# A graph attention kernel: the load of `a` moved to another queue ahead of the first head's weights, and the transposes of the last tile placed one product sooner

## The chip, the cores and the metric

The kernel runs on one core of one Trainium2 chip. The metric is the device time of the whole kernel in microseconds (us). The kernel before took 2300.03 us, the median of four runs (2299.52 to 2300.47).

A core has five engines that run side by side and wait for each other through semaphores: PE (matrix products; PEld is its loading of weights, which overlaps with products), DVE and ACT (elementwise work; ACT also does exponentials), POOL (elementwise work on SBUF) and SP (which only issues transfers). ACT and POOL issue transfers too. The profile numbers the transfer queues: q1 is SP's, q10 is ACT's, q0 is POOL's. All of them feed the same 16 DMA engines.

## The reference

The input `x` has 128 batches of 64 nodes with 512 features, `adj` is a 64 x 64 mask, and all arithmetic is float32. Cut to what matters:

```
h = relu(layernorm(x))
# four heads
Wh = einsum('bnf,hfo->bhno', h, W_heads)              # W_heads [4, 512, 512]
e = leaky(Wh @ a[:, :512] (rows) + Wh @ a[:, 512:] (columns))   # a_heads [4, 1024]
attn = softmax(where(adj > 0, e, -1e9))
h1 = elu(attn @ Wh), heads side by side               # [128, 64, 2048]
# one head
out = elu(the same with W_out [2048, 512] and a_out)
y = relu(out @ w1 + b1) @ w2 + b2 + out
result = x + layernorm(y) * gamma + beta
```

The scores need only `h @ (W a)`, so the kernel folds `a` into the weights first: eight columns `W_h a` for the four heads and the two halves of `a`.

## The kernel before

The 8192 rows of `x` are worked in 64 tiles of 128 rows, and these in 16 groups of four tiles. In a group, PE first does the projections of the four heads (`project1`, line 289 for its matmuls), then the output head's product (`project2`, line 304), and beside it the feed-forward layers of the group before. The products are done by a scheme with seven partial products, so sums of weight blocks are made once on POOL (`weight_sums`), written to DRAM and read back piece by piece (`piece`, line 220).

The first group is different, and the change lies there. Its heads are done with plain products, `head_w(m, j)` (line 629: four matmuls by head m's weights for tile j, which the profile counts as eight), because the blocks of weights are not summed yet. The order in the code is written out by hand at the end of the kernel (from line 852 on) and a scheduler keeps it on each engine by and large: an engine works its instructions strictly in order.

What happens at the start, by name:

- `load(t)` (line 107) brings tile t of `x` through SP's queue. `X[0]` is issued first, then `ar`, then `X[1]` to `X[3]`.
- `ar` (lines 112 to 114) is a 128 x 512 tile, zeroed by DVE; its first eight rows are then loaded with the two halves of `a` for each of four heads (8 rows of 2 KB, 16 KB).
- `fetch(m)` (lines 163 to 169) loads a whole weight matrix of 1 MB, `pw` in the profile. Head 0's goes through ACT's queue, heads 1 to 3 through SP's, the later ones through POOL's. In the text they are called pw0, pw1, pw2, pw3. An argument `after` makes the issue wait for another instruction, by the helper `behind` (line 73), which adds a dependence through a semaphore.
- `norm1(t)` makes the layer norm's statistics on DVE (lines 326 to 332), two small steps on POOL (334, 344) and `hn` by one activation on ACT (346).
- `spread_a(m)` (line 177) spreads two rows of `ar` over all partitions by two products with a column of the identity; they need `ar`. `fold(m, ab)` (line 188) multiplies pw m by them on DVE and sums into the columns of `wa`.
- `transpose_h(t)` (lines 362 and 364) transposes tile t of `hn` by four small PE matmuls into `pth` and copies it to `hT` on ACT. `head_w(m, t)` needs that copy.
- `masks()` (lines 137 to 153) makes small tables on DVE, held behind the last fold: among them `isq` and `hsf`.
- `project_f(0)` (line 372) multiplies `wa` by the four `hT` and spreads the result by ACT into `L` (line 380) and `R` (385), which need `isq` and `hsf`. `scores1(0)` (405) and the softmax follow.

PE's order there is: spread_a(0), transpose_h(0), spread_a(1), head_w(0,0), transpose_h(1), spread_a(2), head_w(0,1), transpose_h(2), spread_a(3), head_w(0,2), transpose_h(3), head_w(0,3), head_w(1,0), project_f(0), head_w(1,1), scores1(0), and so on.

Each transfer through SP's and ACT's queues takes the next of eight semaphores, so an issue waits until the transfer that had the same semaphore before it has landed.

Of the kernel before, what the change touches and what calls it, by code (L numbers as in the profile page):

```python
# [22 lines left out]
def gat_preln_kernel(  # L23
# [30 lines left out]
    nc = tc.nc  # L54
    P = 128
    B, N, F = x.shape
    H = W_heads.shape[0]
    O = W_heads.shape[2]
# [21 lines left out]
    def bank(name):  # L80
        return ps.tile([P, 2, T], FP, tag="mm", name=name)

    def flat(ap):
        return ap.rearrange("p a b -> p (a b)")

    def behind(ins, after, reason):
        tc.add_manual_dep(
            ins.ins, after.ins.name,
            mybir.DependencyInfo(mybir.DependencyClass.Sync, mybir.DependencyReason.DATA),
            reason=reason,  # L90
        )

    def aux(shape, name):
        return ps.tile(shape, FP, tag="aux", name=name, bufs=2)
# [16 lines left out]

    ar = wk.tile([P, O], FP, tag="elu", name="ar", bufs=3)
    nc.vector.memset(ar, 0.0)
    nc.sync.dma_start(out=ar[0:2 * H], in_=a_heads.rearrange("h (r p) -> (h r) p", p=O))
    for t in range(1, G):
        X[t] = load(t)
    aj = const.tile([P, N], mybir.dt.int32, name="aj")
# [45 lines left out]
    def fetch(m, after=None):  # L163
        MT[m] = big.tile([P, KC, O], FP, tag=homes[m], name=f"pw{m}")
        queue = nc.scalar if m == 0 else nc.sync if m < H else nc.gpsimd
        ins = queue.dma_start(out=MT[m], in_=mats[m].rearrange("(k p) o -> p k o", p=P))
        if after is not None:
            behind(ins, after, "not in front of what is needed first")
        return ins

    def spread_a(m, after=None):

        ab = []
        for c in range(2):
            pb = flat(bank(f"pab{m}_{c}"))
            r = 2 * m + c
            ins = nc.tensor.matmul(pb, ident[:, r:r + 1].to_broadcast([P, P]), ar, start=True, stop=True)
            if after is not None:
                behind(ins, after, "not in front of it")
            ab.append(pb)  # L180
        return ab

    def fold(m, ab):

        for c in range(2):
            for k in range(KC):
                junk = wk.tile([P, O], FP, tag="t", name=f"jk{c}_{m}_{k}")
                LAST["fold"] = nc.vector.scalar_tensor_tensor(
                    junk, MT[m][:, k, :], 1.0, ab[c], ALU.mult, ALU.mult,
                    accum_out=wa[:, k, c * H + m:c * H + m + 1],  # L190
                )

    def weight_sums(m, after=None):

        w = MT[m]
        b11, b12 = w[:, 0:2, 0:Q], w[:, 0:2, Q:O]
        b21, b22 = w[:, 2:4, 0:Q], w[:, 2:4, Q:O]
        tag = ("ot", "rt")[m % 2]
        s = [big.tile([P, 2, 2, Q], FP, tag=f"{tag}{i}", name=f"pt{m}_{i}") for i in range(2)]
        free = [nc.gpsimd.tensor_tensor(s[0][:, 0], b12, b11, ALU.subtract)]  # L200
        nc.gpsimd.tensor_tensor(s[0][:, 1], b22, s[0][:, 0], ALU.subtract)
        free.append(nc.gpsimd.tensor_tensor(s[1][:, 0], b22, b12, ALU.subtract))
        for ins in free if after is not None else ():
            behind(ins, after, "the sums come behind it")
        last = nc.gpsimd.tensor_tensor(s[1][:, 1], b21, s[0][:, 1], ALU.subtract)
        TC[m] = [dram.tile([P, 2, 2, Q], FP, name=f"tc{m}_{i}") for i in range(2)]
        for i in range(2):
            nc.gpsimd.dma_start(out=TC[m][i], in_=s[i])
        return last
# [149 lines left out]
    def transpose_h(t):  # L359
        pt = aux([P, KC, P], f"pth{t}")  # L360
        for k in range(KC):
            LAST["th"] = nc.tensor.transpose(pt[:, k, :], HN[t][:, ts(k, P)], ident)
        HT[t] = wk.tile([P, KC, P], FP, tag="hT", name=f"hT{t}", bufs=4)
        LAST["hT"] = nc.scalar.copy(HT[t], pt)
# [261 lines left out]
    def head_w(m, j):  # L626
        pb = aux([P, O], f"hw{m}_{j}")
        for k in range(KC):
            LAST["pe"] = LAST["hw", m, j] = nc.tensor.matmul(
                pb, HT[j][:, k, :], MT[m][:, k, :], start=k == 0, stop=k == KC - 1  # L630
            )
        nc.scalar.copy(flat(HW[j][:, m]), pb)
# [217 lines left out]


    for m in range(H):
        fetch(m)
    nc.vector.memset(wa, 0.0)
    norm1(0)
    ab = spread_a(0)
# [14 lines left out]
    head_w(0, 1)  # L871
    transpose_h(2)
    fold(3, spread_a(3, LAST["pe"]))
    weight_sums(1, LAST["nb"])
    weight_sums(2, LAST["nb"])
    head_w(0, 2)
    transpose_h(3)
    head_w(0, 3)
    masks()
    head_w(1, 0)  # L880
# [150 lines left out]
```

## Time and profile before

| | us |
|---|---|
| median of four runs | 2300.03 |
| the profiled execution | 2299.52 |
| its span on the core | 2297.5 |
| PE busy in the span | 2274.5 |
| DVE busy | 1280.5 |
| POOL busy | 1018.6 |
| ACT busy | 904.4 |
| DMA engines, mean rate over the span | 157 GB/s |
| DMA engines, mean rate 6.49 to 36 us | 341 GB/s |

The profile is of one execution. A row of the timeline gives the start, the length, the engine, the line of the code, the operation, what it writes and reads, and in brackets how long the engine had been idle before and what ended that. The length of a matmul row holds its passage through the array, so rows of PE overlap; the distance of the starts tells the pace. A row of the waits gives the waiting engine and line, what it waited for, the total in us, how many times, and the longest.

Transfers of the first 40 us, with the time from issue to landing:

```profile
pw<-in_L_gnn_W_heads_dram SPq DMA_DIRECT2D x3, 1024.0 KB, 10.2
x<-in_x_dram SPq DMA_DIRECT2D x8, 256.0 KB, 6.0
pw<-in_L_gnn_W_heads_dram ACTq DMA_DIRECT2D x1, 1024.0 KB, 6.3
ar<-in_L_gnn_a_heads_dram SPq DMA_DIRECT2D x1, 16.0 KB
```

Their issues:

```profile
0.72 0.47 ACTq L166 DMA_DIRECT2D pw<-in_L_gnn_W_heads_dram  x1
0.73 0.39 SPq L107 DMA_DIRECT2D x<-in_x_dram  x1
1.41 0.36 SPq L114 DMA_DIRECT2D ar<-in_L_gnn_a_heads_dram  x1
1.81 1.36 SPq L107 DMA_DIRECT2D x<-in_x_dram  x3
3.22 4.17 SPq L166 DMA_DIRECT2D pw<-in_L_gnn_W_heads_dram  x3
```

### The profile page before, as it was taken

How to read it: one execution, taken by the hardware profiler on the slowest of the kernel's cores; microseconds unless marked ns; L12 is line 12 of the kernel's file. 1: busy time of each engine (PE TensorE's matmuls, PEld its weight loads, DVE VectorE, ACT ScalarE, POOL GpSimd, SP SyncE). 2: the span in 40 equal slices, each digit the busy share in tenths (PEclk: the TensorE clock that was granted, in tenths of full speed). 3: DMA queues.
4: the chain of work that ended last, by engine and by line, in shares of the span. 5: the costliest groups of instructions: out<-in, count | busy, mean ns of one | idle time of the engine just before them, and what ended most of it. 6: DMA issues, size and time to landing. Idle time of an engine off the chain costs nothing. (4 is left out here: it accounts for less than half of the span.)

```text
span 2297.5 us, 33255 instructions
## 1 busy us (share of the span) xinstructions
PE 2274.5 (99%) x11856; PEld 1890.6 (82%) x11856; DVE 1280.5 (56%) x2226; ACT 904.4 (39%) x1633; POOL 1018.6 (44%) x906
## 2 busy tenths in 40 slices
PE   8999999999999999999999999999999999999997
PEld 4688888888888888888888888888888888888885
DVE  7555554755546555564655546555475554744427
ACT  3435344252442525335253352534425244251512
POOL 7653534435254442644425344353444525533324
PEclk9999999999999999999999999999999999999999
DMA  7554464644546455464544645446464454635543
GB/s 280 197 179 132 145 180 132 183 133 143 178 132 184 136 152 165 133 184 133 163 152 140 181 134 177 132 146 180 132 181 133 145 176 131 184 118 169 162 146 106
DMA packets 255011, 361.14 MB, mean 157 GB/s; under 512 B 23768, under 2 KB 143608, under 8 KB 254848
## 3 DMA queue, kind: packets, MB, share of 16 engines
q1 hardware_dynamic: 249744, 341.16, 49.2%
q0 software_dynamic: 4576, 16.81, 2.0%
q8 instruction: 96, 1.57, 0.3%
q10 hardware_dynamic: 528, 1.05, 0.1%
q14 instruction: 67, 0.55, 0.1%
HBM read 331.66 MB, written 27.26 MB: 156 GB/s over the span
## 5 line engine op out<-in xcount | busy, mean ns | idle before, releaser
L304 PE MATMUL g_b<-w,h 128*128 128x256 f32 x2560 | 593.1, 379 | 0.0
L304 PEld LDWEIGHTS g_b<-w,h 128*128 128x128 f32 x2560 | 481.1, 190 | 64.6 <-issue 2.0
L289 PE MATMUL g_a<-z,w 128*128 128x256 f32 x1440 | 341.7, 380 | 0.0
L289 PE MATMUL g_a<-zs_z,w 128*128 128x256 f32 x1440 | 336.0, 381 | 0.0
L289 PEld LDWEIGHTS g_a<-zs_z,w 128*128 128x128 f32 x1440 | 269.9, 190 | 59.2 <-issue 24.3
L289 PEld LDWEIGHTS g_a<-z,w 128*128 128x128 f32 x1440 | 272.3, 190 | 41.4 <-DVE g_a L603 5.0
L304 PE MATMUL g_b<-w,hS 128*128 128x256 f32 x1024 | 238.2, 379 | 0.0
L607 POOL TENSOR_TENSOR hS<-hS,h 128x512 f32<-128x512 f32 x60 | 78.1, 1302 | 360.3 <-DVE hS L573 360.3
L304 PEld LDWEIGHTS g_b<-w,hS 128*128 128x128 f32 x1024 | 192.1, 190 | 25.0 <-issue 0.2
L571 ACT ACTIVATE exc<-g_a 128x512 f32<-128x512 f32 x240 | 142.6, 594 | 164.9 <-DVE g_a L603 97.2
L573 DVE SCALAR_TENSOR_TENSOR h<-exc,g_a 128x512 f32<-128x512 f32 x180 | 123.5, 686 | 140.7 <-ACT exc L572 140.1
L572 ACT ACTIVATE exc<-exc 128x512 f32<-128x512 f32 x240 | 151.4, 631 | 6.6
L688 POOL TENSOR_TENSOR h<-h,h 128x512 f32<-128x512 f32 x64 | 86.8, 1364 | 138.6 <-PE g_b L304 138.6
L688 POOL TENSOR_TENSOR h<-hS,h 128x512 f32<-128x512 f32 x64 | 81.6, 1276 | 146.3 <-PE g_b L304 146.0
L314 POOL TENSOR_TENSOR zs_z<-zS,z 128x512 f32<-128x512 f32 x60 | 85.2, 1420 | 134.3 <-PE g_a L289 131.0
L489 ACT COPY at<-s1pt 128x512 f32<-128x512 f32 x64 | 34.4, 590 | 272.1 <-PE s1pt L485 272.1
L830 POOL TENSOR_TENSOR xr<-xr,bs 128x512 f32<-128x512 f32 x64 | 96.6, 1513 | 80.0 <-DMA xr<-in_x_dram 52.4
L304 PE MATMUL g_d<-w,rt 128*128 128x256 f32 x512 | 121.8, 380 | 2.2 <-DVE o L822 1.0
L289 PE MATMUL g_c<-ot,w 128*128 128x256 f32 x512 | 122.8, 383 | 0.6 <-DVE ot L792 0.6
L289 PE MATMUL g_a<-zS,w 128*128 128x256 f32 x480 | 113.4, 379 | 0.0
L304 PEld LDWEIGHTS g_d<-w,rt 128*128 128x128 f32 x512 | 96.9, 190 | 17.4 <-DVE o L822 2.3
L712 DVE SCALAR_TENSOR_TENSOR jf<-wh,ao 128x512 f32<-128x512 f32 x128 | 97.4, 797 | 23.8 <-ACT wh L694 23.6
(164 smaller groups left out, 3538.2 us busy)
## 6 DMA issues: line engine op xcount, KB each, us to landing
w<-tc SPq DMA_DIRECT2D x624, 256.0 KB, 2.8
w<-in_L_gnn_W_out_dram SPq DMA_DIRECT2D x192, 256.0 KB, 2.8
w<-in_L_gnn_W_heads_dram SPq DMA_DIRECT2D x180, 256.0 KB, 3.2
w<-in_L_gnn_w_dram SPq DMA_DIRECT2D x96, 256.0 KB, 2.8
x<-in_x_dram SPq DMA_DIRECT2D x64, 256.0 KB, 4.3
xr<-in_x_dram SPq DMA_DIRECT2D x128, 128.0 KB, 2.7
out_dram<-o SPq DMA_DIRECT2D x128, 128.0 KB, 2.4
tc<-pt POOLq DMA_DIRECT2D x20, 512.0 KB, 4.3
```

The lines of the kernel that those rows point to most:

```text
L289: LAST["pe"] = nc.tensor.matmul(bk[:, o, :], w[:, k, ts(o, P)], a[:, k, :], start=start and o == 0 and k == 0, stop=k == 1, skip_group_che ...
L304: LAST["pe"] = nc.tensor.matmul(bk[:, j, :], a[:, k, ts(j, P)], w[:, k, :], start=start and k == 0 and j == 0, stop=i == len(ms) - 1 and k ...
L314: eng.tensor_tensor(s2, s1, a11, ALU.subtract)
L489: nc.scalar.copy(AT[t].rearrange("p b h n -> p (b h) n"), pt)
L571: nc.scalar.activation(ex, src, AF.Relu, scale=-1.0)
L572: nc.scalar.activation(ex, ex, AF.Exp, scale=-1.0)
L573: nc.vector.scalar_tensor_tensor(dst, ex, -1.0, src, ALU.add, ALU.max)
L607: nc.gpsimd.tensor_tensor(dst, dst, H1["22"][:, h], ALU.add)
L688: nc.gpsimd.tensor_tensor(dst[:, h], x0[:, h], x1[:, h], ALU.subtract)
L712: nc.vector.scalar_tensor_tensor(junk, WH2[g][:, j], 1.0, ao[:, c, :], ALU.mult, ALU.mult, accum_out=f[:, c, j:j + 1],)
L830: nc.gpsimd.tensor_tensor(xr, xr, bs, ALU.add)
```

## The change

The load of `ar` is issued by ACT and not by SP. The load of head 0's weights, also issued by ACT, is made to wait for it. And `transpose_h(3)` is placed ahead of `weight_sums(1)`, `weight_sums(2)` and `head_w(0, 2)`; it stood behind them. What is computed is the same.

```diff
     ar = wk.tile([P, O], FP, tag="elu", name="ar", bufs=3)
     nc.vector.memset(ar, 0.0)
-    nc.sync.dma_start(out=ar[0:2 * H], in_=a_heads.rearrange("h (r p) -> (h r) p", p=O))
+    load_a = nc.scalar.dma_start(out=ar[0:2 * H], in_=a_heads.rearrange("h (r p) -> (h r) p", p=O))
     for t in range(1, G):
         X[t] = load(t)
...
     for m in range(H):
-        fetch(m)
+        fetch(m, load_a if m == 0 else None)
     nc.vector.memset(wa, 0.0)
     norm1(0)
     ab = spread_a(0)
...
     head_w(0, 1)
     transpose_h(2)
     fold(3, spread_a(3, LAST["pe"]))
+    transpose_h(3)
     weight_sums(1, LAST["nb"])
     weight_sums(2, LAST["nb"])
     head_w(0, 2)
-    transpose_h(3)
     head_w(0, 3)
     masks()
```

In the built program the order of instructions differs in these places alone. PE: the four transposes of tile 3 stand ahead of the eight matmuls of head_w(0,2). ACT: the load of `ar` stands first, pw0's second, and the copy of `hT` 3 ahead of the copy of head_w(0,2). SP: the load of `ar` is gone, and the first piece of W_out (line 220) stands ahead of the loads of tiles 5, 6 and 7 of `x`; it stood behind them. DVE: the statistics of tile 1 stand ahead of one small step (line 332) of tile 0.

## The prediction

> **What bounds the kernel now.** I read the page first (busy shares), then PE's idle time by stretches, then the waits of the first 40 us, then the timeline around the two places that the diff touches, and last the DMA queues in that stretch.
>
> ```profile
> PE 2274.5 (99%) x11856; PEld 1890.6 (82%) x11856; DVE 1280.5 (56%) x2226; ACT 904.4 (39%) x1633; POOL 1018.6 (44%) x906
> ...
> 0.00:6.49 6.49, 0.00 (x1) 0.03 (x1) 2.02 (x8) 1.40 (x2) 2.79 (x11) 1.00 0.72 243
> 6.49:36.00 29.51, 28.78 (x72) 13.26 (x72) 27.82 (x91) 7.42 (x12) 22.16 (x26) 1.00 0.96 341
> 36.00:600.00 564.00, 563.53 (x3025) 454.74 (x3024) 315.55 (x543) 234.04 (x431) 272.34 (x250) 1.00 0.53 163
> ...
> PE pab L177 <- DMA ar<-in_L_gnn_a_heads_dram: 6.5, 1, 6.5
> ...
> PE hw L629 <- ACT hT L364: 0.7, 1, 0.7
> ```
>
> The stretches list, after the length, the busy time of PE, PEld, DVE, ACT and POOL. PE is the bound: between 36 and 600 us it is idle for 564.00 - 563.53 = 0.47 us. The front holds two idle pieces: 6.49 us until the first matmul, ended by the landing of `ar`, and 0.73 us (29.51 - 28.78) in one wait, on the copy of a transposed h tile. So whatever brings PE's continuous run forward shifts the rest with it, and the two pieces are an upper limit of what this diff can give.
>
> ```profile
> 6.49 3.75 PE L177 MATMUL pab<-ar,ident 128*128 128x512 f32 x4 [6.49 <-DMA ar<-in_L_gnn_a_heads_dram]
> ...
> 10.03 1.06 PE L362 MATMUL pth<-ident,hn 128*128 128x128 f32 x4
> ...
> 10.89 2.29 PE L177 MATMUL pab<-ar,ident 128*128 128x512 f32 x4
> ...
> 13.02 3.60 PE L629 MATMUL hw<-pw,hT 128*128 128x512 f32 x8
> ...
> 27.63 0.60 PE L362 MATMUL pth<-ident,hn 128*128 128x128 f32 x4
> ...
> 28.31 0.59 ACT L364 COPY hT<-pth 128x512 f32<-128x512 f32 x1
> 28.95 0.30 PEld L629 LDWEIGHTS hw<-pw,hT 128*128 128x128 f32 x2 [0.96 <-ACT hT L364]
> ```
>
> From 6.49 to 13.02 PE works without a break: spread_a(0), the transposes of tile 0, spread_a(1), then head_w(0,0). That is 6.53 us. The weight loads of spread_a(0) start 0.86 apart, the last two of spread_a(1) 0.43 apart (11.73, 12.16), so the first 5.2 us ran at half pace, though the granted clock is printed as 1.00 there.
>
> **Part 2, transpose_h(3) before head_w(0,2).** Nothing is added or removed: four transposes and one copy change places with eight matmuls, and the copy of hT3 now comes before the copy of hw on ACT. Before, the transposes at 27.63 were followed by head_w(0,3), which needs their copy (28.31 + 0.59 = 28.90). At the sister place, tile 1, unrelated matmuls follow the transposes 0.44 later (16.45 to 16.89). So head_w(0,3) could start at 28.07 and starts at 28.95: 0.87 us (0.73 by the wait row, 0.96 by the weight loads' row). After, hT3's copy lies beside the 3.43 us of head_w(0,2); without that cover it would cost the same 0.87. hn3 is there since 13.69 + 0.81 = 14.5, and head_w(0,2) itself needs hT2, copied at 22.72 + 0.59 = 23.3, while it starts at 24.19. I take -0.87.
>
> **Part 1, `ar` on ACT's queue, the first head's weights (pw0) behind it.** Removed from SP: one issue of 0.36 us and its wait for the memset, so x1 to x3 are issued 0.7 us sooner. Added on ACT: that issue, at 1.41 as before (the memset ends at 0.90 + 0.48), and a wait: the built program lets pw0's issue wait for the landing of `ar`, not only for its issue. Queued behind that wait on ACT: pw0 (0.47), the table load (1.28) and hn0. Who waits for pw0: fold(0) on DVE, weight_sums(0) on POOL and head_w(0,0) on PE. One more thing moves: pw3's issue on SP waited for the landing of pw0 (7.02), since the two share a semaphore; in the changed program x0 has that place, so pw3 is issued at about 4.2.
>
> Landing of `ar`. Issue to landing is 2.4 us at the fastest kind of row (the output rows) and 3.4 us for x0 (0.73 to 4.13). 1.41 + 2.4 = 3.8 to 1.41 + 3.4 = 4.8; I take 4.1, x0's own time, since both are served by engines that have just started. Before it was 6.4, because:
>
> ```profile
> DMA packets 368, 0.74 MB, mean 370 GB/s; under 512 B 7, under 2 KB 7, under 8 KB 368
> ...
> q10 hardware_dynamic: 355, 0.73, 100.2%
> q1 hardware_dynamic: 13, 0.01, 3.3%
> ```
>
> This is 3 to 5 us; q10 is ACT's queue (pw0 alone), q1 is SP's. pw0 held all 16 engines while `ar` and three x tiles, issued from 1.41 on, stood still. PE's 6.53 us of work can then end at 4.1 + 6.5 = 10.6. hn0 is no later than before: x0 lands no later, the table load ends at 4.2 + 0.5 + 1.3 = 6.0, hn0 was written from 6.37 on.
>
> Landing of pw0. Issued at 4.15, first packets 1.1 later (x0: issued 0.73, its first packets at the end of the window 0 to 2): 5.25. By 5.0 the DMA engines moved 1.03 MB (0.05 + 0.24 + 0.39 + 0.35 by 1 us windows), the four x tiles; so pw1 (1.05 MB) has just begun. If the queues take turns, or pw0 waits for pw1 alone, both are through after 2.1 MB at 0.378 MB per us: 5.05 + 5.55 = 10.6, and landed 0.45 later (pw0 before: last packets 6.6, landed 7.0): 11.05. If pw0 goes first, 5.25 + 2.8 + 0.45 = 8.5. If the transfers are served in the order of issue, pw0 stands behind pw2 (13.9) or behind pw3 too (16.6). The near case is the first: between 24 and 27 us two queues with work share the engines (66.8% and 37.5%). I take 11.1, so head_w(0,0) starts at 11.2 and not at 13.02: -1.8 us (bounds -2.4 by PE's own 10.6, +3.7 by 16.7).
>
> The Trainium skill, DMA: Bandwidth & Descriptors, section Queues, rings and completion order, says that each DMA engine takes turns between queues packet by packet, some 9 to 17 descriptors at a time and at most 64. The rows of 3 to 5 us above show no turns within the one transfer of pw0, which by that rule must have been one packet; by the rule the sum is the 11.1 case. Against the change speaks the same rule: what pw1 has begun on an engine is finished as one packet before pw0 gets its turn there.
>
> Where the rest goes. fold(0) started at 10.74, held by DVE's own statistics, and now waits for pw0: 11.15, 0.4 later; so does everything DVE does up to the masks.
>
> ```profile
> 33.67 0.38 DVE L147 TENSOR_SCALAR isq<-isf,par 128x2 f32<-128x2 f32 x2
> ...
> 37.17 0.81 ACT L380 ACTIVATE L<-pf,isq 128x128 f32<-128x128 f32 x2 [0.46 <-PE pf L372]
> ```
>
> isq is then ready at 34.05 + 0.41 = 34.46, and PE's pf at 37.10 - 2.67 = 34.43. A tie: 3 us of slack are used up, nothing is lost yet (0 to 0.1), and scores1, at 40.66 - 2.67 = 38.0, has R at 34.5 + 2.3 = 36.8. The next place where DVE meets PE is the softmax, 41.79 - 2.67 = 39.1, where DVE is free at 38.11 + 0.41 = 38.5. weight_sums(3) on POOL (44.80) follows ACT's hn, and that PE; it shifts along.
>
> **Sum.** -1.8 - 0.87 + 0 = -2.7 us. Against the profiled execution's own time (2299.52 us, span 2297.5 and 2.0 around it) that is 2296.8. That execution is the lowest of the four, 0.5 under their median of 2300.03; against the median it is 2297.4, -0.12%.
>
> **Rivals.** About 0.2% (4.6 us) is what a measurement here tells from no change.
> - Forecast, turns between the queues: -2.7; with PE's own bound and a shorter half-paced stretch down to -4.2, with a late `ar` (4.8: pw0 at 11.8) and 0.73 up to -1.9. 2295.8 to 2298.2.
> - pw0 behind pw1 and pw2: landing 13.9, head_w(0,0) at 14.0, +1.0 - 0.87 = +0.1, 2300.2; up to 2302 if PE's pace falls in the 3.4 us that it stands (10.6 to 14.0). For it: before, x0, pw0, `ar` went strictly in order of issue. Against it: 24 to 27 us.
> - The slower side, pw0 behind pw1, pw2 and pw3: it lands at 16.6, PE stands from 10.6 to 16.7, head_w(0,0) starts 3.7 later; less 0.87 that is +2.8. If PE falls back to half pace it loses what the start lost: 5.2 us at half pace, 2.6. The only long idle stretch in this trace, before 6.49, was followed by it, so +5.2 is nearer: 2305.2, at the least 2302.8. It decides from a landing after 13.0 + 0.87 = 13.9. For it: pw3 is no longer held back. The Trainium skill, TensorE: Matmul & The Clock Gate, part The HAM clock gate, puts the fall at one idle window of about 3.4 us and the warm-up at about the same; by 3.4 us of half pace the price is +2.8 + 1.7 = +4.5, where the start here took 5.2 us.
> - The change starts PE sooner and the DVE chain (fold, masks, isq) or a later due time takes it back: about 2300. For it: the tie above. Against it: the slacks worked out, all positive.
>
> **How the numbers follow.** Forecast 0.64, behind two 0.13, behind three 0.13, taken back 0.07, something faster than -4.6 us 0.03. Time: 2297.4. Range: from 2295.6 (the forecast's own low end and a little) to 2302.0, which takes in the second and fourth case and leaves out the third and the last (0.16). The forecast's own range is 2295.8 to 2298.2. Faster by over 0.2%: 0.03. Slower: the third case's upper part, 0.08. Within: 0.89.
>
> **What would show it.** First spread matmul at 4.1 (3.8 to 4.8) and not 6.49; pw0's packets on q10 beside those of q1 from 5.2 to 10.6; head_w(0,0) at 11.2 with PE idle before it for under 1 us, ended by the DMA of pw0; no wait for hT3 before head_w(0,3), which starts at 26.3; ACT's first L at 34.5, PE's pf and DVE's isq within 0.3 us of each other. Wrong would be a head_w(0,0) later than 13.0, weight loads 0.86 apart behind it, or a new PE wait between 34 and 60 us.

## The result and the profile after

| | median, us | runs | lowest to highest | ratio to before, 95% interval |
|---|---|---|---|---|
| before | 2299.72 | 54 | 2298.32 to 2301.17 | |
| changed | 2303.55 | 34 | 2301.18 to 2305.74 | 1.0017 [1.0012, 1.0022] |

The changed kernel is 3.8 us slower, where 2.7 us less were forecast. The difference is small, but the interval is clear of 1. The profiled execution took 2305.74 us with a span of 2302.7; it is the highest of the 34, so its stretches show the loss at its largest: +5.2 us of span.

The stretches of the changed kernel (start and end, length, then busy time of PE, PEld, DVE, ACT, POOL, the granted clock, the DMA share and GB/s):

```profile
0.00:6.49 6.49, 1.97 (x3) 0.97 (x4) 2.98 (x11) 1.56 (x2) 2.79 (x11) 1.00 0.65 193
6.49:36.00 29.51, 23.36 (x59) 10.76 (x58) 20.86 (x70) 6.77 (x11) 20.69 (x24) 0.88 0.92 330
36.00:600.00 564.00, 563.53 (x3012) 452.05 (x3011) 315.57 (x558) 231.10 (x426) 270.96 (x252) 1.00 0.52 163
```

Up to 6.49 PE now works 1.97 us where it worked none. From 6.49 to 36 it is idle for 6.15 us (29.51 - 23.36), where it was idle for 0.73, and the granted clock of that stretch (the third figure from the end) is 0.88. From 36 us on the idle time is the old one, 0.47. So all of the loss is in the front, and this is where, in PE's timeline and its weight loads:

```profile
4.52 3.75 PE L177 MATMUL pab<-ar,ident 128*128 128x512 f32 x4 [4.52 <-DVE n1mv L330]
8.06 0.86 PE L362 MATMUL pth<-ident,hn 128*128 128x128 f32 x4
8.76 1.88 PE L177 MATMUL pab<-ar,ident 128*128 128x512 f32 x4
16.80 6.37 PE L629 MATMUL hw<-pw,hT 128*128 128x512 f32 x8 [6.16 <-DMA pw<-in_L_gnn_W_heads_dram]
23.01 0.60 PE L362 MATMUL pth<-ident,hn 128*128 128x128 f32 x4
...
41.58 1.08 PE L372 MATMUL pf<-hT,wa 128*32 128x128 f32 x32
...
18.64 0.34 PEld L629 LDWEIGHTS hw<-pw,hT 128*128 128x128 f32 x1 [0.52 <-issue]
19.49 0.34 PEld L629 LDWEIGHTS hw<-pw,hT 128*128 128x128 f32 x1 [0.52 <-issue]
...
25.16 0.19 PEld L629 LDWEIGHTS hw<-pw,hT 128*128 128x128 f32 x1 [0.24 <-issue]
25.59 0.19 PEld L629 LDWEIGHTS hw<-pw,hT 128*128 128x128 f32 x1 [0.24 <-issue]
```

The first product starts at 4.52 (it was 6.49). The profile puts the end of this wait down to a statistics step of DVE, which the product does not read; `ar` had landed by 4.40, when the issue of pw0, which waits for it, began. PE is through with what does not need pw0 at 16.80 - 6.16 = 10.64. Then it waits for pw0. head_w(0,0) starts 3.78 us later than before (16.80, 13.02) and takes 6.21 us to the transposes of tile 1 (16.80 to 23.01) instead of 3.43: its weight loads stand 0.85 apart, those of head_w(0,1) 0.43. That is 2.78 more. The granted clock in windows of 1 us shows the same:

```profile
14.00:15.00 1.00, 0.00 (x0) 0.00 (x0) 0.00 (x0) 0.00 (x0) 0.00 (x0) 1.00 1.05 387
15.00:16.00 1.00, 0.00 (x0) 0.00 (x0) 0.00 (x0) 0.00 (x0) 0.00 (x0) 0.71 1.06 389
16.00:17.00 1.00, 0.20 (x1) 0.23 (x2) 0.23 (x1) 0.00 (x0) 0.20 (x1) 0.50 1.05 385
...
21.00:22.00 1.00, 1.00 (x2) 0.34 (x1) 1.00 (x5) 0.00 (x0) 1.00 (x2) 0.50 1.08 357
22.00:23.00 1.00, 1.00 (x3) 0.43 (x2) 1.00 (x5) 0.00 (x0) 1.00 (x2) 0.88 1.08 357
```

The clock fell to half at about 15.4, while PE stood, and was whole again at about 22.2 (worked out from 0.71 and 0.88). From the transposes of tile 1 to project_f it is 0.99 shorter, since head_w(0,3) no longer waits. 3.78 + 2.78 - 0.99 = 5.57, and project_f starts at 41.58, 5.56 after the old 36.02.

The issues on ACT, and the queues of the DMA engines from 6 to 7 us, from 10 to 12 us and from 14 to 16 us (packets, MB, share of 16 engines; q1 is SP's, q10 ACT's):

```profile
1.42 0.57 ACTq L114 DMA_DIRECT2D ar<-in_L_gnn_a_heads_dram  x1
4.40 0.42 ACTq L166 DMA_DIRECT2D pw<-in_L_gnn_W_heads_dram  x1
...
q1 hardware_dynamic: 150, 0.29, 99.6%
...
q1 hardware_dynamic: 212, 0.42, 54.2%
q10 hardware_dynamic: 194, 0.40, 51.1%
...
q1 hardware_dynamic: 352, 0.70, 94.5%
q10 hardware_dynamic: 46, 0.08, 10.8%
```

pw0 is issued at 4.40 and not at 0.72. Its data do not move before 8 us, while the engines work almost for SP's queue alone (POOL's has 5.2% at most from 5 to 8 us). From 10 to 14 us it gets half of them, and its last packets come after 14 us.

### The profile page after: what moved, and what is told of

It is laid out like the page before. It is cut to its first block, busy times and chain, and to the rows that moved or that the text cites. A ratio compares the mean times of both kernels' runs of the same rounds, so it can differ in the third digit from the quotient of the medians.

```text
span 2302.7 us, 33254 instructions
## 1 busy us (share of the span) xinstructions
PE 2276.5 (99%) x11856; PEld 1891.3 (82%) x11856; DVE 1275.0 (55%) x2226; ACT 904.5 (39%) x1633; POOL 1018.6 (44%) x906
```

## The experiments

All are compared with the kernel before in the same session on the same chip; e7 to e9 ran in a later session on another chip. A common list first; the third column is where the profiled execution started head_w(0,0).

| run | what it is | head_w(0,0) | median, us (before) | ratio, 95% interval |
|---|---|---|---|---|
| e1_part2 | transposes moved, nothing else | 12.17 | 2298.16 (2299.47) | 0.9995 [0.9986, 1.0004] |
| e2_part1 | load of `a` moved, nothing else | 15.19 | 2304.66 (2299.47) | 1.0021 [1.0012, 1.0030] |
| e3_order_only | both, pw0 not waiting for the landing | 12.85 | 2298.58 (2299.47) | 0.9994 [0.9986, 1.0003] |
| e4_warm | changed kernel, PE kept busy in the wait | 16.77 | 2302.03 (2299.47) | 1.0012 [1.0003, 1.0021] |
| e5_hold_sp | changed kernel, SP's large loads behind pw0 | 11.72 | 2297.62 (2299.69) | 0.9990 [0.9981, 1.0000] |
| e6_rows8 | both, eight-row products, no memset, pw0 waiting for nothing | 11.94 | 2300.68 (2299.69) | 1.0004 [0.9995, 1.0013] |
| e7_part2_warm | transposes moved, PE brought to pace first | 10.39 | 2296.46 (2299.50) | 0.9986 [0.9977, 0.9996] |
| e8_rows8_warm | e6 with full-height products first | 15.09 | 2302.13 (2299.50) | 1.0010 [1.0001, 1.0019] |
| e9_rows8_fill | e6 with an eight-row product in the gap | 13.19 | 2302.06 (2299.50) | 1.0012 [1.0003, 1.0020] |

**The two parts apart.**

```diff
# e1: the load of a and the order of the fetches as before
     fold(3, spread_a(3, LAST["pe"]))
+    transpose_h(3)
...
     head_w(0, 2)
-    transpose_h(3)
```

> Only the transposes of tile 3 are moved; the load of a stays on SP's queue. Theory (the move gains the wait for hT3, the load of a loses all the rest): no wait of head_w(0,3) on hT3, 0.87 us less than before, about 2298.9 where before is 2299.7. Rival (the move costs something, by the copy of hT3 ahead of the copy of head_w(0,2)): no gain or a loss, 2299.7 or more.

> Only the load of a is moved to ACT's queue, with pw0 waiting for its landing; the transposes stay where they were. Theory: the changed kernel's time plus the 0.87 us that the move of the transposes gives, about 2304.4, with pw0 landing near 16.7 us. Rival (the two parts disturb each other): near the changed kernel's 2303.6 or below it.

e1 is 1.3 us less, e2 5.2 us more than before. In e2 pw0 landed at 15.1, earlier than the 16.7 that was expected. The ratio's interval of e1 still touches 1, but its 11 runs (2297.72 to 2298.67) lie below the median of before. PE's timeline of e1 shows the wait gone: the transposes run right into 24 matmuls of head_w.

```profile
21.63 1.88 PE L177 MATMUL pab<-ar,ident 128*128 128x512 f32 x4
23.35 0.60 PE L362 MATMUL pth<-ident,hn 128*128 128x128 f32 x4
23.78 10.46 PE L629 MATMUL hw<-pw,hT 128*128 128x512 f32 x24
```

From head_w(0,0) to project_f it takes 34.18 - 12.17 = 22.01 us, before 36.02 - 13.02 = 23.00: the move of the transposes is worth 0.99, and the difference of e2 and the changed kernel (2304.66 and 2303.55) agrees. The parts do not disturb each other; the loss is the first part's alone.

**The wait for the landing.** pw0's issue waits for the memset of the tile and not for the landing of `a`; ACT then issues the one right after the other.

```diff
-    nc.vector.memset(ar, 0.0)
+    zero_a = nc.vector.memset(ar, 0.0)
...
-        fetch(m, load_a if m == 0 else None)
+        fetch(m, zero_a if m == 0 else None)
```

> As the changed kernel, but pw0's issue waits for the memset of the tile and no longer for the landing of a: ACT issues a and pw0 one right after the other, near 1.4 and 2.0 us. Theory (the loss is the wait for the landing, which puts pw0 behind SP's large loads): pw0 lands by 10 us, first spread matmul at 4.5, head_w(0,0) at 11.0, 2.0 earlier than before; less 0.9 for the transposes, about 2296.8. Rival 1 (a transfer on ACT's queue always comes behind those that SP has in flight): pw0 lands at 13 or later, 2300 or more. Rival 2 (the order on ACT's queue holds a up): first spread matmul after 6 us, 2299.

PE's timeline of e3, ACT's issue of pw0, and the DMA queues from 5 to 6 us:

```profile
4.42 3.75 PE L177 MATMUL pab<-ar,ident 128*128 128x512 f32 x4 [4.42 <-DVE n1mv L330]
12.85 3.67 PE L629 MATMUL hw<-pw,hT 128*128 128x512 f32 x8 [2.40 <-DMA pw<-in_L_gnn_W_heads_dram]
...
2.03 0.44 ACTq L166 DMA_DIRECT2D pw<-in_L_gnn_W_heads_dram  x1
...
q10 hardware_dynamic: 99, 0.20, 55.5%
q1 hardware_dynamic: 69, 0.12, 38.8%
```

2298.58, 5.0 less than the changed kernel (4.7 when each is set against the kernel before of its own session): the wait is the cause. But the size was missed: pw0 landed at 12.8 and not by 10, and PE still stood for 2.40 us. That landing is close to rival 1's 13, but pw0 was not behind SP's loads: the last two rows show the two queues from 5 to 6 us, pw0's with 55.5% of the engines. The time is no better than that of the moved transposes alone. PE kept its full pace over those 2.40 us (3.51 us from 12.85 to the transposes at 16.36).

**What stands beside pw0.** SP's three large loads wait for pw0's landing; the first four pieces of W_out and the rows loaded behind them wait for the last of the three, so that they do not move ahead.

```diff
     for m in range(H):
-        fetch(m, load_a if m == 0 else None)
+    first = fetch(0, load_a)
+    for m in range(1, H):
+        LAST["pw"] = fetch(m, first)
...
+        if len(HELD) < 4:
+            HELD.append(p)
+            behind(ins, LAST["pw"], "not in front of the heads")
...
```

> As the changed kernel, but SP's loads of pw1 to pw3, and the pieces and rows behind them, wait for the landing of pw0, so that pw0 has the DMA engines for itself from its issue at 4.4 us on. Theory (pw0 lands late because SP's large loads are ahead of it and beside it): pw0 lands at 9 to 10 us, head_w(0,0) at 10.7 with PE at full pace, 2296.5 to 2297.5. Rival (the wait on the landing of a costs by itself): pw0 lands after 13 us all the same, 2300 or more. What could spoil it: pw1 is needed by fold(1) 4.9 us after fold(0) begins and lands 4 to 5 us after pw0.

Its timeline (SP's issues, PE) and q10 from 7 to 8 us:

```profile
11.61 1.49 SPq L166 DMA_DIRECT2D pw<-in_L_gnn_W_heads_dram  x3
...
11.72 3.67 PE L632 MATMUL hw<-pw,hT 128*128 128x512 f32 x8 [0.79 <-DMA pw<-in_L_gnn_W_heads_dram]
...
q10 hardware_dynamic: 177, 0.36, 105.5%
```

With the same late issue (4.28) pw0 now has all engines from 7 to 8 us, and landed at 11.6, 5.1 earlier than in the changed kernel. 2297.62, just above the expected 2296.5 to 2297.5. From issue to landing the same transfer took 6.3 us in the kernel before, 12.3 in the changed kernel and 7.3 here: of the 6.0 us more, 5.0 are SP's loads ahead of it and beside it. It is not all, and the landing missed the expected 9 to 10: the last 58 of its 528 packets came between 9 and 12 us, when its queue took 12.7%, 13.7% and 2.2% of the engines and SP's nothing. Why these were late no view here tells.

**PE's pace.** Seven products nobody reads fill the wait of the changed kernel.

```diff
-    fold(1, spread_a(1, LAST["th"]))
+    ab1 = spread_a(1, LAST["th"])
+    warm = flat(bank("warm"))
+    for _ in range(7):
+        LAST["warm"] = nc.tensor.matmul(warm, ident, ar, start=True, stop=True)
+    fold(1, ab1)
```

> As the changed kernel, with seven more products of the identity and the tile of a, into a bank that nobody reads, between spread_a(1) and head_w(0,0): 7 x 0.86 us, which fill PE's wait for pw0 (10.6 to 16.8). Theory (about half of the loss is PE's pace after the wait): head_w(0,0) starts at 16.8 as before but its weight loads are 0.43 apart and not 0.86, 2.8 us less than in the profiled changed kernel, and 1.5 to 2.8 less than its median: 2300.8 to 2302.0. Rival (the loss is the late landing alone, the pace is set by something else that is slow after 16.8, such as the reads of pw0): weight loads still 0.86 apart, no change of the time, 2303.6.

```profile
10.76 6.17 PE L869 MATMUL warm<-ar,ident 128*128 128x512 f32 x14
16.77 3.60 PE L629 MATMUL hw<-pw,hT 128*128 128x512 f32 x8
20.20 0.60 PE L362 MATMUL pth<-ident,hn 128*128 128x128 f32 x4
```

head_w(0,0) starts at the same time, 16.77, and takes 3.43 us again; project_f follows at 38.78, 2.80 earlier than in the changed kernel's profile. By the medians it is 1.5 us less than the changed kernel (2302.03, 2303.55), or 1.3 when each is set against the kernel before of its own session: the low end of the 1.5 to 2.8 expected, or just short of it. The profiled execution of the changed kernel is the slowest of its 34. So the pace is a part of the loss by itself, and it comes from PE's standing still, not from what it reads.

**`a` and pw0 both early.** The spread products read the eight loaded rows only, so there is no memset to wait for, and pw0's issue waits for nothing.

```diff
-    nc.vector.memset(ar, 0.0)
...
-            ins = nc.tensor.matmul(pb, ident[:, r:r + 1].to_broadcast([P, P]), ar, start=True, stop=True)
+            ins = nc.tensor.matmul(
+                pb, ident[0:2 * H, r:r + 1].to_broadcast([2 * H, P]), ar[0:2 * H], start=True, stop=True
+            )
...
-        fetch(m, load_a if m == 0 else None)
+        fetch(m)
```

> As the changed kernel, but the spread products read only the eight rows of a that are loaded (identity and a cut to 8 rows), so the memset and the wait for it go, and pw0's issue waits for nothing. ACT issues a at 0.7 and pw0 at 1.2. Theory: a lands at 3.5 or before, first spread matmul at 3.5, PE ready for head_w(0,0) at 10.0, pw0 landed by 8; 3.0 + 0.9 us less than before, 2295.8. Rival (a and pw0 come so early that x0 is late, or a waits behind other transfers): first spread matmul after 5 us, or the transposes of tile 0 late by hn0, 2298 or more.

This fell, and the reasons given for the rival are not what cost most. `a` was there before 2.49 us and pw0 held nobody up; hn0 held the transposes of tile 0 by 0.92 us. But PE ran at half pace until about 18 us, so that head_w(0,0) started 1.94 later than expected and took 6.39 us and not 3.43:

```profile
2.49 3.78 PE L176 MATMUL pab<-ar,ident 8*128 8x512 f32 x4 [2.49 <-POOL ident masks.py:199]
...
8.23 3.77 PE L176 MATMUL pab<-ar,ident 8*128 8x512 f32 x4
11.94 6.56 PE L630 MATMUL hw<-pw,hT 128*128 128x512 f32 x8
```

Two runs ask why; both add to e6 only products into an unread bank.

```diff
# e8: in front of spread_a(0)
+    for _ in range(9):
+        nc.tensor.matmul(warm, ident, ident, start=True, stop=True)
# e9: behind spread_a(0)
+    nc.tensor.matmul(warm, ident[0:2 * H, 0:1].to_broadcast([2 * H, P]), ar[0:2 * H], start=True, stop=True)
```

> The same eight-row kernel without the identity products, with one more eight-row product after spread_a(0), which fills PE's gap of 0.9 us before the transposes of tile 0 (6.3 to 7.2). Theory (eight-row products do not bring the pace up): weight loads 0.86 apart until after 17 us all the same, 2300.7 or a little more. Rival (it was the gap): full pace from 8 us on, head_w(0,0) at 10.5, 2297.

> The spread products with eight rows and no memset, a and pw0 issued on ACT at 0.7 and 1.3, as in the run before of that kind, but with nine products of the identity with itself, all 128 rows, in front of spread_a(0) (2.5 to 6.4). Theory (products of eight rows do not bring PE's pace up, so that head_w(0,0) ran at half pace until 18 us): spread_a(0) after 6.4 at 0.43, head_w(0,0) at 10.4 at full pace, 2296 to 2297. Rival (the pace was low for another reason, such as the reads of pw0): head_w(0,0) still 0.86 apart, 2300 or more.

e9: with the gap shorter than 0.2 us, PE ran some 9 us of eight-row products, 0.86 from weight load to weight load, and the transposes of tile 0 between them, and head_w(0,0) went on at 0.86 until 17.6. The gap is out. The time, 2302.06, is 1.4 above e6, since the added product lets head_w(0,0) start later (13.19, 11.94). e8 missed its number and came out at its rival's, but not for the rival's reason: the spread products, which do not read pw0, were at half pace already. Its nine full-height products lasted from 2.48 to 6.4 at half pace, and the eight-row products behind them stayed there:

```profile
2.48 4.21 PE L859 MATMUL warm<-ident 128*128 128x128 f32 x18 [2.48 <-POOL ident masks.py:199]
6.62 3.78 PE L176 MATMUL pab<-ar,ident 8*128 8x512 f32 x4
...
15.09 5.41 PE L630 MATMUL hw<-pw,hT 128*128 128x512 f32 x8
```

The products of head_w(0,0), with full-height weights, then came to 0.43 at 18.6, 3.5 us after they began. In the three eight-row kernels PE reached full pace only when head_w(0,0) had run for 3.5 to 6 us. In e7 below the same nine products have full-height ones behind them, and PE is at full pace from 6.5 us on. That height is what counts is the reading that fits these runs; another property of the eight-row products (they read fewer rows and change fewer weights) was not tried apart, nor a longer run of full-height ones in front of them.

**The better kernel.** Part 2 alone, the load of `a` where it was, and the nine full-height products in front of spread_a(0), which reads all 128 rows there.

> The moved transposes alone (the load of a stays on SP's queue, as before), and nine products of the identity with itself in front of spread_a(0), into a bank that nobody reads: 9 x 0.43 us from 2.5, when the identity is made, to 6.4, when a lands. Theory (the start is worth its pace: PE loses up to 2.6 us there by running at half pace until 11.7): weight loads of spread_a(0) 0.43 apart, head_w(0,0) at 10.4, 2.6 + 0.9 less than before, 2296.2 where before is 2299.7, and 1.2 to 2 less than with the moved transposes alone. Rival 1 (hn0 or hT0 holds head_w(0,0)): 11 us or later, 2297 or more. Rival 2 (small products do not bring the pace up): as with the moved transposes alone, 2298.2.

```profile
2.49 4.19 PE L858 MATMUL warm<-ident 128*128 128x128 f32 x18 [2.49 <-POOL ident masks.py:199]
6.49 1.91 PE L177 MATMUL pab<-ar,ident 128*128 128x512 f32 x4
...
8.67 1.88 PE L177 MATMUL pab<-ar,ident 128*128 128x512 f32 x4
10.39 3.60 PE L629 MATMUL hw<-pw,hT 128*128 128x512 f32 x8
```

head_w(0,0) starts at 10.39, as forecast. The time is 2296.46, 0.3 above the expected 2296.2; against the kernel before it is 3.0 us less, where 3.5 were expected. The changed kernel, in its own session, is 7.1 above it. PE starts on `ar` at the same 6.49 as before and does the same work in 3.90 us that took 6.53 before and 5.66 in e1.

## Why the prediction was wrong

- **Landing of `ar`**, 4.1 (3.8 to 4.8): the first product started at 4.52, 4.20, 4.42, 4.43 and 4.40 in the five kernels with it on ACT and the memset. Right.
- **PE's 6.53 us of work end at 10.6**: 10.64, but by luck. The work began 0.4 us later than the 4.1 that was taken and lasted 6.12 us (10.64 - 4.52), 0.4 less, because full pace came sooner.
- **Part 2, -0.87**: -0.99 by the profiles, -1.1 and -1.3 by the medians of two pairs. Right.
- **Landing of pw0, 11.05, "I take 11.1, so head_w(0,0) starts at 11.2".** This step failed, and with it the sign. It landed at 16.7 (in e4 too; in e2, with the same loads, at 15.1). The term that was mis-sized most is the 2.1 MB for pw0 and pw1 together: it took no account of pw2 and pw3, which SP had issued by 4.1. From 10 to 14 us pw0 shared the engines half and half with SP's queue (51.1% and 54.2% from 10 to 12). By 14 us that queue had moved 3.03 MB: if it works in the order of issue, that is four tiles of x, pw1 and nine tenths of pw2. Of pw0's 528 packets 48 were then still to come, two of them after 16 us. The start was off to the same side: the x tiles were put through by 5.0, by the old rates of 1 us windows, but those rates held pw0's own traffic. Without it 0.84 MB were moved by 5.0 and not 1.03 (0.03 + 0.27 + 0.31 + 0.23 by 1 us windows), 0.81 of them by SP's queue, and DVE got x3 at 7.1. By 8 us 1.72 MB had been moved, with pw1 some six tenths through and none of pw0. An estimate from these windows: with nothing behind pw1 in SP's queue, pw0 and pw1 would have been through when 3.2 MB were, near 11.9, and pw0 landed near 12.3. So the late start is worth some 1.3 us of the miss, and pw2, pw3 and the late last packets some 4.4. The row that was read as "turns", 24 to 27 us, shows sharing between SP's queue and POOL's; what was missed is that sharing goes on with the next transfer in the other queue, so the later one gets half a rate for as long as the other queue holds work.
- **The slower rival** (pw0 behind pw1 to pw3, landing 16.6, 2302.8 to 2305.2) had the place and the price. It had the landing by luck: pw0 was not behind pw3, of which SP's queue had moved nothing when nine tenths of pw0 were there, if it works in the order of issue. The rival was given 0.13. Its term of 2.6 us for the pace measured 2.78 in the profiled execution and 1.5 by the medians of e4 and the changed kernel. The stated range ended at 2302.0, below the measured 2303.55.
- The tie of DVE's masks and PE's pf was not reached: pf came at 41.6, isq had been ready at 37.65. In e7, where PE is 3.6 us earlier than before at that point (32.40, 36.02), the time still fell by 3.0 us, of 3.5 forecast.

The prediction quoted the Trainium skill, DMA: Bandwidth & Descriptors, section Queues, rings and completion order: engines take turns between queues packet by packet. The half shares from 10 to 14 us agree with it. From 5 to 8 us no turns show: pw0, issued at 4.40, moved nothing while SP's queue had 86 to 100% of the engines, whereas in e5, issued at 4.28 with little left in SP's queue, its first packets came between 5 and 6 us. The prediction's own sentence against the change, that what pw1 has begun is finished first, would fit, but no view here shows where such a packet ends. Its other page, TensorE: Matmul & The Clock Gate, part The HAM clock gate, says that PE falls to half pace after at least one idle window of about 3.4 us, and comes back after at least one busy window of that length. The runs agree: in the changed kernel the granted clock fell some 4.8 us after PE stood still (10.64, 15.4) and came back some 5.4 us after head_w(0,0) began; in e2, which stood for 5.50 us, it fell after some 4.1. After standing 2.40 and 0.79 us head_w(0,0) took 3.51 us, at full pace (e3, e5). The 5.4 us lie near the 5.2 of the start, from which the slower rival's price was worked out.

## What to carry to other kernels

A wait for a small transfer's landing, put in front of a large one, costs far more than the wait: pw0 issued at 0.72 landed at 7.0, at 2.03 at 12.8, at 4.40 at 16.7 (one execution each). What is asked is what the other queues will have issued by then, all of it and not only the next transfer. And where PE must wait some us for data, look at its pace behind the wait as well as at the idle time: filling the 4 us before the first product with products that nobody reads made this kernel 1.7 us faster than the moved transposes alone.

## What was not expected of the hardware

Products with eight rows left PE at half pace for as long as they lasted (some 9 us in e9), and head_w behind them began at that pace. Once PE was at full pace, they kept it: behind head_w(0,0) in e6, at 18.86, their weight loads stand 0.43 apart.

A transfer of 1 MB that had the DMA engines nearly alone (e5) took 7.3 us from issue to landing, against 6.3 for the same transfer at the kernel's very start. And SP's queue alone moved only 0.23 to 0.29 MB per us from 4 to 7 us in the changed kernel, where 0.35 to 0.37 had been moved with pw0 in it.
